# Attention results finished with longer planned lags, and their divisors broadcast by one transfer in place of four

## The chip, the cores and the metric

The kernel runs on one core of one Trainium2 chip. The time is device microseconds (us) of that core. Engines: TensorE (PE) does the matmuls, VectorE (DVE) elementwise work and row reductions, ScalarE (ACT) activations and copies, GpSimd (POOL) some elementwise work and DMA issue, and SyncE (SP) only issues DMAs. Each engine runs its own instructions in program order.

## The reference

x is 2 × 1024 × 512 in fp32. Cut to what matters:

```python
xn = layernorm(x)                                   # over the last 512
q, k, v = split(xn @ w_qkv.T + b_qkv)               # 32 heads of 16
scores = q @ k.T / 4 + slope[h] * (key - S + 1)     # ALiBi
attn   = softmax(where(causal, scores, -1e9))
s = (attn @ v).reshape(B, S, D) @ w_out.T + b_out
h = silu(oct_linear(xn, w_gate)) * oct_linear(xn, w_up)   # 512 -> 1360, ternary octonion weights
g = silu(oct_linear(h, w_down))
out = x + s * g
```

The octonion linear layers use weights rounded to −1, 0 or 1 times a scale, in an 8 × 8 pattern of signed blocks.

## The kernel before

**Units.** Attention is cut into 32 units (b, g, qc): two batches, eight groups of four heads, two halves of 512 queries. A unit has four parts on TensorE: score matmuls with queries on the partitions, of which VectorE takes row maxima (L566, tiles `s` and `s_d`, `left`, `mx`); the maxima turned round and put into `q_stack` as extra rows; score matmuls with keys on the partitions (L682, L701), whose exponentials ScalarE takes into `p` (L69 in the profile, since all engines but TensorE record through one helper at that line); and value matmuls (L720), which add up in the PSUM tile `po`. The values carry a column of ones, so that in each head's 32 rows of `po` row 16 is the softmax sum of its queries. ScalarE copies a finished `po` to `posb`.

**A result's steps.** `finish(b, g, qc)` (L733) returns six steps, written for one unit:
- `sums`: a DMA from SyncE takes the four rows of sums out of `posb` into `l`, 128 partitions × 16 (`l<-posb`);
- `invert`: VectorE takes the reciprocal, `rl`;
- `keep`: a DMA puts `rl` into DRAM as 4 × 512 (`ld<-rl`);
- `spread`: DMAs bring each head's row of 512 factors back to its 32 partitions of `r`, 128 × 512 (`r<-ld`);
- `divide`: VectorE multiplies `posb` by `r`, in place in `r`;
- `store`: a DMA writes `r` to `att` in DRAM (`att<-r`). Later `oT<-att` fetches it for the output projection.

**The order of work.** The program is written out by a planner at build time. It keeps modelled times in ns: `now` for TensorE, `act` and `dve` for the others. In each turn of its main loop it may emit a fill of keys or queries (`try_fill`, four DMAs `k_stack<-sp` or `q_stack<-sp`, SyncE), then one due step of a result (`do_chores`), then a fetch of `oT` (`try_fetch`), then one group of matmuls (`step`). Each step of a result is a triple (emit, cost on VectorE, lag): after it is emitted, the next is due when its modelled end plus the lag has passed:

```python
emit, cost, lag = steps.pop(0)
emit()
end = run_dve(now[0], cost) if cost else now[0]
chores[n] = (end + lag, steps, u)
if not steps:
    stored[units[u]] = end + lag
```

So the lags do not wait on the chip; they decide where in each engine's program the step stands. On the chip an engine waits, at that place, until the step's inputs are there, and what follows it on that engine waits too. SyncE's program also has the loads of x (`xt`), of the query and key weights (`wqr`), the spills `sp<-st` of the projections, and the fills.

**Buffers.** `posb` has two buffers, `l` and `rl` one each. `r` has the tag "ot" with two buffers, which it shares with `md`, the transposed pieces of the down weights (`turn_down`: PE transposes to `ptd`, ScalarE copies `md<-ptd`, GpSimd stores `mw<-md`), made between 120 and 180 us.

**After attention** a feed-forward loop runs (gate and up matmuls `pg`, `pu` at L1455, down matmuls `pd` at L1497). Steps of results that are left by then are emitted one round per pass of that loop.

Of the kernel before, what the change touches and what calls it, by code (L numbers as in the profile page):

```python
# [75 lines left out]
def kernel(  # L76
# [21 lines left out]
    act_, dve_, pool_, sp_ = (  # L98
        InOrder(tc, engine, held) for engine in (nc.scalar, nc.vector, nc.gpsimd, nc.sync)
    )  # L100
# [12 lines left out]
    dram = ctx.enter_context(tc.tile_pool(name="dram", bufs=1, space=DRAM))  # L113
# [111 lines left out]
    for n in range(2):  # L225
        pool_.dma_start(
            out=bqk_sb[n * 64 : n * 64 + 64, 1 - n : 1 - n + 2 * NG],
            in_=bqk.rearrange("(i d) c -> i d c", d=32)[:, 0:HD, :],
# [504 lines left out]
    def finish(b, g, qc):  # L733


        posb = po_tiles.pop((b, g, qc))
        key = f"{b}_{g}_{qc}"
        box = {}

        def sums():  # L740
            box["l"] = wk.tile([P, 16], F32, tag="l", name=f"l_{key}", bufs=1)
            sp_.dma_start(
                out=box["l"],
                in_=posb[HD:P:32, :].rearrange("h (a n) -> h a n", n=16),
            )

        def invert():
            box["rl"] = wk.tile([P, 16], F32, tag="rl", name=f"rl_{key}", bufs=1)
            dve_.reciprocal(box["rl"], box["l"])

        def keep():
            box["dram"] = spill.tile([4, 512], F32, tag="l", name=f"ld_{key}")
            sp_.dma_start(
                out=box["dram"].rearrange("h (a n) -> (h a) n", n=16), in_=box["rl"]
            )

        def spread():
            box["r"] = wk.tile([P, 512], F32, tag="ot", name=f"r_{key}")
            for h in range(4):
                sp_.dma_start(  # L760
                    out=box["r"][32 * h : 32 * h + 32],
                    in_=box["dram"][h : h + 1].to_broadcast([32, 512]),
                )

        def divide():
            dve_.tensor_tensor(box["r"], posb, box["r"], ALU.mult)

        def store():
            sp_.dma_start(out=att[b, g, :, qc * 512 : qc * 512 + 512], in_=box["r"])


        return [
            (sums, 0, 9000),
            (invert, 250, 300),
            (keep, 0, 3500),
            (spread, 0, 7000),
            (divide, 620, 300),
            (store, 0, 4500),
        ]

# [85 lines left out]
    for b in range(B):  # L866
        for hh in range(2):
            n = 2 * b + hh
# [11 lines left out]
        for gp in range(2 - 2 * b, NP):  # L880
            n = b * NP + gp
# [374 lines left out]
    def next_value():  # L1256
        if V[0] == len(vals) or V[0] not in p_ready or not V[0] and S_[0] < head_v:
            return []
        u, n, cell = vals[V[0]]
        last = 4 * units[u][2] + 2  # L1260

        def go():
            value_step(*units[u], n, cell)
            V[0] += 1
            run_pe("V", ready, sum(w * 1.668 + 40 for _, _, w in cell))
            if n == last:
                o_free[0] = run_act(now[0] + START, 480) + END
                chores.append((o_free[0], finish(*units[u]), u))

        ready = max(p_ready[V[0]], o_free[0] if n == 0 else 0)  # L1270

        if n % 2 == 0 and n < last and V[0] + 2 >= E_cell():
            ready = max(ready, p_ready.get(V[0] + 1, HELD) - 800)
        return [(ready, 0, 0, go)] if ready < HELD else []
# [377 lines left out]
```

## Time and profile before

| | |
|---|---|
| median of 3 runs | 1032.09 us (1031.54 to 1032.76) |
| the profiled execution | 1030.97 us |
| its span | 1029.1 us |
| mean granted TensorE clock | 0.991 |
| PE, DVE, ACT, POOL busy | 988.5, 581.4, 490.6, 171.7 us |
| DMA queue of SyncE | 74384 packets, 111.40 MB |
| r<-ld | 128 issues, 64 KB each |

The span runs from the profile's first to its last instruction; the execution's own time has 1.87 us more around it. A line such as `r<-posb,r` names the tile written and the tiles read, without their numbers; times in the timeline count from the start of the span. Busy time of one engine lies beside that of the others. What an engine waited for is put down to what came last. The granted clock is the share of full speed at which TensorE was let run.

### The profile page before, as it was taken

What the parts mean: (1) busy time and instruction counts of PE and PEld (TensorE: products, weight loads), DVE (VectorE), ACT (ScalarE), POOL (GpSimd) and SP (SyncE); (2) the same over time, 40 slices, a digit from 0 to 9 for tenths busy, and PEclk for the clock granted to TensorE, in tenths of its full rate; (3) what the DMA queues carried; (4) which work ended last, traced back from release to release, by engine and by line L of the source; (5) the groups of instructions that cost most, each with busy time, mean ns of one, the idle gap of its engine ahead of it and who ended that gap; (6) DMA issues with size and microseconds to landing.
All of it is one profiled execution on the core that took longest, in us unless ns stands there. A gap on an engine that the chain in (4) does not pass through costs nothing. (4 is left out here: it accounts for less than half of the span.)

```text
span 1029.1 us, 15486 instructions
## 1 busy us (share of the span) xinstructions
PE 988.5 (96%) x5290; PEld 669.1 (65%) x5290; DVE 581.4 (56%) x1726; ACT 490.6 (48%) x942; POOL 171.7 (17%) x289
## 2 busy tenths in 40 slices
PE   8999988999999999899999999989999999999996
PEld 6655645775666676656667656545476678788784
DVE  6588945776577675676766757748251132231312
ACT  4034456756656554456654556556761132232322
POOL 7701023100200200010010000010021133232322
PEclk9999998999999999999999999999999999999998
DMA  5854735244454423433533244532242113030201
GB/s 203 244 150 154 169 129 167 63 131 154 144 150 138 137 66 123 152 109 117 166 95 96 84 130 148 124 100 79 86 148 82 51 66 109 1 123 1 94 29 42
DMA packets 77935, 117.16 MB, mean 114 GB/s; under 512 B 19624, under 2 KB 29488, under 8 KB 77856
## 3 DMA queue, kind: packets, MB, share of 16 engines
q1 hardware_dynamic: 74384, 111.40, 35.1%
q0 software_dynamic: 3424, 4.64, 1.6%
q8 instruction: 42, 0.69, 0.3%
q14 instruction: 37, 0.30, 0.1%
q10 hardware_dynamic: 48, 0.13, 0.0%
HBM read 77.77 MB, written 37.56 MB: 112 GB/s over the span
## 5 line engine op out<-in xcount | busy, mean ns | idle before, releaser
L69 ACT ACTIVATE p<-s 128x512 f32<-128x512 f32 x576 | 319.4, 596 | 183.4 <-PE s L701 105.7
L682 PE MATMUL s<-q_stack,k_stack 128*128 128x512 f32 (+3 forms) x768 | 263.0, 408 | 4.9 <-ACT p L69 4.5
L69 DVE TENSOR_REDUCE left<-s 128x1 f32<-128x512 f32 x256 | 161.4, 681 | 71.2 <-PE s L566 70.9
L682 PEld LDWEIGHTS s<-q_stack,k_stack 128*128 128x128 f32 x768 | 132.4, 191 | 88.3 <-ACT p L69 44.2
L69 DVE CUSTOM_DVE_ANT_0 nowhere<-s_d,mask 128x384 uint8<-128x384 f32 (+2 forms) x384 | 139.6, 419 | 21.4 <-PE s_d L566 20.0
L720 PE MATMUL po<-p,v 128*32 128x512 f32 (+3 forms) x1536 | 142.6, 491 | 2.8 <-ACT p L69 2.8
L566 PE MATMUL s_d<-k_stack,q_stack 126*128 126x384 f32 (+3 forms) x512 | 128.5, 348 | 4.0 <-DVE mx L69 3.6
L479 PE MATMUL pqk<-xnT,wq 128*128 128x512 f32 x256 | 128.3, 601 | 3.2 <-ACT md L69 1.2
L69 POOL DMA_DIRECT2D q_stack<-mr x64 | 31.0, 488 | 558.5 <-ACT mr L69 558.5
L69 DVE SCALAR_TENSOR_TENSOR h<-pu,sc_u,sg 128x512 f32<-128x512 f32 (+1 forms) x44 | 33.0, 750 | 152.2 <-PE pu L1455 146.7
L566 PEld LDWEIGHTS s_d<-k_stack,q_stack 126*128 126x128 f32 x512 | 83.4, 192 | 26.4 <-DVE mx L69 11.2
L69 DVE CUSTOM_DVE_ANT_0 s_d<-s_d,mask 128x512 f32<-128x512 f32 x128 | 85.6, 715 | 21.9 <-PE s_d L566 21.6
L566 PE MATMUL s<-k_stack,q_stack 126*128 126x512 f32 x256 | 86.5, 422 | 7.9 <-DMA q_stack<-sp 5.7
L69 POOL TENSOR_TENSOR hs<-h,hs 128x512 fp32r<-128x512 f32 (+1 forms) x43 | 56.2, 1307 | 211.6 <-ACT hs L69 211.6
L720 PEld LDWEIGHTS po<-p,v 128*32 128x32 f32 x1536 | 43.4, 109 | 72.6 <-issue 57.9
L701 PE MATMUL s<-mask_r,ident_r 128*128 128x256 f32 (+1 forms) x320 | 89.7, 280 | 0.0
L69 ACT ACTIVATE sg<-pg,sc_g 128x512 f32<-128x512 f32 (+1 forms) x44 | 30.2, 687 | 104.4 <-PE pg L1455 104.4
L69 ACT CAST hs<-h 128x512 fp32r<-128x512 f32 (+1 forms) x44 | 27.3, 620 | 84.4 <-DVE h L69 84.4
L439 PE MATMUL pv<-wv,xnT 128*128 128x256 f32 x256 | 65.1, 384 | 0.0
L701 PEld LDWEIGHTS s<-mask_r,ident_r 128*128 128x128 f32 x320 | 61.1, 191 | 2.8 <-issue 1.7
L566 PEld LDWEIGHTS s<-k_stack,q_stack 126*128 126x128 f32 x256 | 47.1, 190 | 23.6 <-issue 5.8
L479 PEld LDWEIGHTS pqk<-xnT,wq 128*128 128x128 f32 x256 | 44.5, 190 | 27.2 <-issue 18.6
(149 smaller groups left out, 1152.0 us busy)
## 6 DMA issues: line engine op xcount, KB each, us to landing
sp<-st SPq DMA_DIRECT2D x32, 512.0 KB
k_stack<-sp SPq DMA_DIRECT2D x128, 128.0 KB
q_stack<-sp SPq DMA_DIRECT2D x128, 128.0 KB
wqr<-in_wqk_dram SPq DMA_DIRECT2D x16, 512.0 KB
r<-ld SPq DMA_DIRECT2D x128, 64.0 KB
att<-r SPq DMA_DIRECT2D x32, 256.0 KB
xt<-in_x_dram SPq DMA_DIRECT2D x16, 256.0 KB
oT<-att SPq DMA_DIRECT2D x32, 128.0 KB
```

The source lines that it names most:

```text
L69: ins = issue(*args, **kwargs)
L439: nc.tensor.matmul(ps[:, 0:256], lhsT=xnT[:, c, b * S + kt * P : b * S + (kt + 1) * P], rhs=wv_tiles[2 * b + hh][:, c, :], start=(c == 0), ...
L479: nc.tensor.matmul(ps, lhsT=wq_tiles[b, gp][:, kt, which, :], rhs=xnT[:, kt, b * S + c * 512 : b * S + (c + 1) * 512], start=(kt == 0), st ...
L566: nc.tensor.matmul(ps, lhsT=q_of(b, g, qc)[0 : NR - 2, h, tl * P : (tl + 1) * P], rhs=k_of(b, g, c)[0 : NR - 2, h, :n], start=True, stop=True,
L682: nc.tensor.matmul(ps[:, c0 : c0 + w], lhsT=k_of(b, g, kt // 4)[0:NR, h, kt % 4 * P : (kt % 4 + 1) * P], rhs=q[0:NR, h, 512 - w : 512], st ...
L701: pe(nc.tensor.matmul(out, lhsT=ident_r, rhs=rhs, start=False, stop=True))
L720: nc.tensor.matmul(po[32 * i : 32 * i + 32, 512 - w : 512], lhsT=v[:, kt, h * VC : h * VC + 32], rhs=p[:, i * part + c0 : i * part + c0 + ...
```

## The change

The four transfers of `spread` become one, with a source whose leading size is 4 (heads), then 32 repeats of a row, then 512. Three planned lags grow: after `invert` from 300 to 2000 ns, after `spread` from 7000 to 8000, after `divide` from 300 to 2500. The planned time from the copy of `po` to `stored` grows from 25.47 to 30.37 us. Each later step so stands later in the engines' programs, and the planner's later choices move with it.

```diff
         def spread():
             box["r"] = wk.tile([P, 512], F32, tag="ot", name=f"r_{key}")
-            for h in range(4):
-                sp_.dma_start(
-                    out=box["r"][32 * h : 32 * h + 32],
-                    in_=box["dram"][h : h + 1].to_broadcast([32, 512]),
-                )
+            sp_.dma_start(
+                out=box["r"],
+                in_=box["dram"].rearrange("h (e n) -> h e n", e=1).to_broadcast([4, 32, 512]),
+            )
...
         return [
             (sums, 0, 9000),
-            (invert, 250, 300),
+            (invert, 250, 2000),
             (keep, 0, 3500),
-            (spread, 0, 7000),
-            (divide, 620, 300),
+            (spread, 0, 8000),
+            (divide, 620, 2500),
             (store, 0, 4500),
         ]
```

## The prediction

> **What bounds the kernel now.** First I read the page's first part, then the chain that ended last.
>
> ```profile
> PE 988.5 (96%) x5290; PEld 669.1 (65%) x5290; DVE 581.4 (56%) x1726; ACT 490.6 (48%) x942; POOL 171.7 (17%) x289
> PE 4%; issue 0%; DVE 0%; ACT 0%; DVEq 0%
> ```
>
> TensorE is busy for 96% of the span; VectorE has nearly half its time free. So an edit of VectorE's and SyncE's steps can gain only what TensorE now idles or runs at a lower clock, and can lose only by making new idle time. The recovered chain covers only the last 4%, so I looked for TensorE's idle time stage by stage.
>
> ```profile
> 100.00:200.00 100.00, 90.02 (x510) 58.45 (x512) 66.23 (x204) 61.20 (x131) 19.19 (x33) 0.95 0.47 135
> 400.00:500.00 100.00, 97.22 (x560) 61.13 (x559) 69.31 (x219) 57.59 (x106) 5.78 (x16) 0.98 0.43 132
> 835.00:1029.10 194.10, 183.99 (x806) 148.68 (x804) 53.26 (x60) 52.30 (x82) 55.64 (x42) 0.99 0.16 55
> ```
>
> Columns: stretch, length, busy time of PE, PEld, DVE, ACT and POOL, granted clock, DMA share, GB/s. From 100 to 200 us 10 us are idle at a clock of 0.95: that stretch is the softest. The last stretch is the feed-forward loop, one matmul stream behind another; there only its start, 749.79 us (the first pg), can move. It lasts 279.3 us in both programs: by the timeline the last stores land 7 us or more before their oT is fetched.
>
> Next, who waits for the five steps of a chain, by the view of waits (total, times, longest) and then SyncE's queue:
>
> ```profile
> DVE r L69 <- DMA r<-ld: 11.1, 5, 4.1
> PE s L566 <- DMA q_stack<-sp: 5.7, 3, 3.4
> ACT md L69 <- DMA mw<-md: 8.5, 3, 3.3
> SPq L69 <- DVE rl L69: 49.1, 16, 6.8
> SPq L69 <- DVE r L69: 33.5, 15, 6.8
> ```
>
> Of 32 divides 5 wait for their factors. The timeline (start, length, engine; in brackets idle time and releaser) shows what two of them cost:
>
> ```profile
> 91.46 1.98 SPq L69 DMA_DIRECT2D r<-ld  x4
> 95.11 0.69 DVE L69 TENSOR_TENSOR r<-posb,r 128x512 f32<-128x512 f32 x1 [2.73 <-DMA r<-ld]
> 96.46 0.50 PE L566 MATMUL s<-k_stack,q_stack 126*128 126x512 f32 x1 [2.20 <-DVE left L69]
> ...
> 416.87 1.82 SPq L69 DMA_DIRECT2D r<-ld  x4
> 423.49 0.69 DVE L69 TENSOR_TENSOR r<-posb,r 128x512 f32<-128x512 f32 x1 [4.13 <-DMA r<-ld]
> 424.90 0.50 PE L566 MATMUL s_d<-k_stack,q_stack 126*128 126x384 f32 x2 [2.66 <-DVE mx L69]
> ...
> 684.25 0.96 PE L566 MATMUL s<-k_stack,q_stack 126*128 126x512 f32 x3 [3.39 <-DMA q_stack<-sp]
> ```
>
> While a divide waits, the row maxima queued behind it on VectorE wait too, and the score matmuls lack a bank. The first costs TensorE 2.20 us. The second costs 2.66 us and then clock:
>
> ```profile
> 425.00:430.00 5.00, 5.00 (x21) 4.52 (x22) 3.85 (x19) 1.74 (x3) 0.00 (x0) 0.66 0.60 185
> ```
>
> 5 us at 0.66 lose 1.7 us, so this wait costs 4.4 in all. The third gap is a late fill of q_stack and cost no clock.
>
> **The parts of the change.** *One transfer for four.* The rows:
>
> ```profile
> L69 SPq DMA_DIRECT2D r<-ld x128: 303/419/1354, 91.5 to 762.2; - x128
> L69 SPq DMA_DIRECT2D l<-posb x32: 555/587/642, 68.1 to 752.2; - x32
> L69 SPq DMA_DIRECT2D att<-r x32: 320/338/474, 95.8 to 767.4; - x32
> ```
>
> Four issues at the median of 419 ns are 1.68 us per chain. For the new one the bounds are 0.34 (the plain store) and 0.64 us (the longest l<-posb); I take 0.59, as l<-posb too has an access pattern led by four rows. That frees 32 × 1.09 = 35 us of SyncE's queue, which isn't the bound: worth nothing itself, but fills behind it go out earlier.
>
> *How soon it lands.* Now 3.65 us from first issue to the divide (91.46 to 95.11), 1.67 after the fourth issue ended. The mean packet takes 35.1% × 16 × 1029.1 us / 74384 = 78 ns (an estimate from the page's queue row). The 128 rows of 2 KB are 8 packets on each of 16 engines (0.6 us) or, if the transfer is split only over its four leading rows, 32 on each of four (2.5 us). So it lands 0.59 + 1.67 = 2.3 us after issue at best, 2.3 + 1.9 = 4.2 at worst: −1.4 to +0.5 against now. I take the worst, because the broadcast stands with 4 outermost. Either way the extra 1 us of planned lag covers it.
>
> [...] No row here shows a broadcast led by four.
>
> *Longer lags.* The planned chain was 9 + 0.55 + 3.5 + 7 + 0.92 + 4.5 = 25.47 us and becomes 30.37. It needs no more buffers: a unit comes every (752.2 − 68.1)/31 = 22.1 us, posb has two buffers (44 us) and is held some 26, l and rl some 10. The gain meant is that SyncE's keep and store no longer stand waiting (49.1 and 33.5 us above) ahead of fills; off the path, except for the fills.
>
> *What moves where.* The built programs differ in order on every engine. I followed the three gaps into the new order:
> - Gap at 96.46: the divide stands two row maxima later, and TensorE has four score groups and two value groups before it needs that bank. Gain 2.2 (0 to 2.2).
> - Gap at 424.90: these factors are now requested ahead of the 1 MB of wqr loads that they followed (414.93). A landing of 3.65 in place of 6.6 us ends the wait. Gain 4.4 (0 to 4.4).
> - Gap at 684.25: the fill now stands ahead of one store, but still behind the transfers that take until 673.3 to issue. Gain 0.4 (0 to 3.4).
> [...]
> - Stretch 120 to 180 us, where the down weights are transposed: md copies and r tiles share the two buffers of tag "ot". Copies there already wait for each other:
>
> ```profile
> 136.53 0.58 ACT L69 CAST md<-ptd 128x512 fp32r<-128x512 f32 x1 [3.28 <-DMA mw<-md]
> 140.24 0.53 ACT L69 CAST md<-ptd 128x256 fp32r<-128x256 f32 x2 [3.12 <-DMA mw<-md]
> ```
>
> One buffer turns round in 3.7 us. In the new order r_0_1_0 takes its buffer after md_0_4, so SyncE waits there for md_0_4's store, and the store of r_0_0_1, for which md_0_8 waits, is queued behind that. Against it, the exponentials of unit (0,1,1) come some ten places earlier and fill ScalarE's idle time. From −5 (half of the 10 us idle goes) to +6; taken: +1.
> - New waits: the 32 divides meet other neighbours. Today's waits cost 2.2 + 4.4 = 6.6. With lags longer by 1 us I take +2.5 (0 to 6.6).
>
> **The sum**: −2.2 − 4.4 − 0.4 + 1 + 2.5 = −3.5 against the profiled execution's own 1030.97 us (span 1029.1 and 1.87 around it) gives 1027.5. That execution lay 1.12 below the median of 1032.09, so as a median: 1028.6. This case's own range: 1024 to 1032.
>
> **Rivals.** *Slower: the shared buffers.* md_0_8 waits for md_0_4's store (3.7), then the issues of r_0_1_0 and att (0.59 + 0.34), then that store's landing (about 4, as a landing took 3.65): 8.6 us after md_0_4 in place of 3.7. TensorE's next transposes need its PSUM bank: 4.9 idle and 1.7 of clock, +6.6; a second crossing of this kind, at md_2_0, adds up to 3. With the gains: −7.0 + 2.5 + 6.6 to 9.6 = +2.1 to +5.1, median 1034 to 1037; 1041 if the new waits cost all of 6.6. It eats up the gain from a stall of 4.5 us in that stretch, and can be measured as a loss from 6.5. For it: the 3.28 and 3.12 waits. Against it: TensorE has score and value groups to do first.
>
> *Slower: four engines carry too much.* If the factors' 32 packets hold up the fills that share these engines, each by up to 1.9 us, and two fills in the eight groups are as tight as the one at 684, +3.8, and clock once, 1.7: −7.0 + 2.5 + 3.8 + 1.7 = +1.0, and +5.4 if the 4.4 isn't won: median 1033 to 1037. For it, fills were late three times (5.7 us); against it, the DMA share is 0.43.
>
> *No change: the waits move.* Other divides and fills wait in place of these, costing again about 6.6: median 1031 to 1033. For it: both gaps come from where the planner happens to put a step, not from its lags as such.
>
> **How the numbers follow.** Chances: forecast 0.50, shared buffers 0.24, four engines 0.11, no change 0.15. About 0.2% (2 us) is what this kernel's measurement can tell from no change. The range: 1021 (the soft stretch gives its 5 us and little new waits) to 1040. Faster 0.50, same 0.16, slower 0.34.
>
> **What would show it.** Right: r<-ld x32 at about 0.59 us each on SyncE, landing in 4.2; no TensorE idle before 96.5 and 425, and the clock near 425 at 1.00; the first pg near 746. Wrong: ACT md waits well over 8.5 us and a lower share of PE from 100 to 200 (under 88); new DVE r waits above 11.1; or q_stack waits above 5.7.
>
> [...]

## The result, and the profile after

The changed kernel is slower: 1035.02 us median of 15 runs (1032.61 to 1036.98) against 1032.29 of 15 runs before; the ratio is 1.0031, 95% interval 1.002 to 1.0042. The forecast was 1028.6, faster. The time lies in the predicted range, and where two of the rivals were priced: the shared buffers (1034 to 1037) and the four engines (1033 to 1037). The experiments show that the shared buffers are one half of the story; the other half is a term that the prediction had set to nothing.

The profiled execution took 1036.54 us (span 1034.8, clock 0.985). It and the profiled execution before (1030.97) lie 5.6 us apart, twice the 2.7 between the medians; the account of stages below is of these two executions, and its single terms are no surer than that. The windows (stretch, length, busy time of PE, PEld, DVE, ACT, POOL, clock, DMA share, GB/s) first:

```profile
100.00:200.00 100.00, 81.85 (x467) 55.12 (x466) 59.65 (x192) 54.55 (x118) 19.20 (x33) 0.90 0.46 132
425.00:430.00 5.00, 5.00 (x33) 2.55 (x32) 2.95 (x16) 1.97 (x4) 0.00 (x0) 1.00 0.75 268
170.00:175.00 5.00, 5.00 (x26) 4.04 (x29) 1.66 (x9) 4.26 (x10) 1.57 (x3) 0.58 0.26 76
```

The wait at 425 us is gone and its clock is whole, as forecast. The soft stretch got worse: TensorE is busy for 81.85 us there in place of 90.02, at a clock of 0.90 in place of 0.95. The waits (total, times, longest) and the new transfer's row:

```profile
DVE r L69 <- DMA r<-ld: 15.2, 5, 4.1
ACT md L69 <- DMA mw<-md: 13.4, 5, 4.7
ACT md L69 <- DMA att<-r: 9.4, 1, 9.4
```

```profile
L69 SPq DMA_DIRECT2D r<-ld x32: 512/553/746, 91.4 to 766.9; - x32
```

The transfer issues in 0.55 us (0.59 was taken). But the divides wait 15.2 us for it, more than the 11.1 before, in spite of the longer lag. And a copy of md now waits 9.36 us for a store of r. Here is that place in the timeline, ScalarE's copies, SyncE's queue and TensorE's gaps:

```profile
143.49 0.59 ACT L69 CAST md<-ptd 128x512 fp32r<-128x512 f32 x1 [2.17 <-DMA mw<-md]
153.43 0.53 ACT L69 CAST md<-ptd 128x256 fp32r<-128x256 f32 x2 [9.36 <-DMA att<-r]
...
147.22 0.52 SPq L69 DMA_DIRECT2D r<-ld  x1
147.79 0.47 SPq L69 DMA_DIRECT2D att<-r  x1
...
154.36 1.46 PE L373 MATMUL ptd<-ident_r,m_d 128*128 128x128 f32 x4 [5.72 <-ACT m_d L69]
169.02 2.44 PE L373 MATMUL ptd<-ident_r,m_d 128*128 128x128 f32 x8 [5.06 <-ACT m_d L69]
```

r_0_1_0 waits on SyncE until 147.22 for its buffer, which md_0_4 has just left; the store of r_0_0_1 stands behind it, although its divide (139.30, 0.69 us long) ended at 140.0; md_0_8 wants that store's buffer; and ScalarE's signed copies (m_d), for the next transposes, stand behind md_0_8.

Where the time went, stage by stage, from the idle time in brackets on TensorE and, per stretch of 5 us, busy time × (1 − clock):

| stage, us | idle before → after | lost to clock |
|---|---|---|
| 0 to 60 | 7.6 → 7.3 | 0 → 0 |
| 60 to 100, and the clock after it | 2.2 → 1.5 | 0 → 1.6 |
| 100 to 200 | 9.8 → 18.0 | 3.8 → 6.1 |
| 200 to 450 | 3.8 → 0.5 | 1.7 → 0 |
| 450 to 600 | 0 → 1.3 | 0 → 0 |
| 600 to 760 | 6.4 → 4.9 | 0 → 1.5 |

That is 3.7 us more idle time and 3.7 more lost to clock. The first pg moved by only 4.7 (749.79 to 754.50): some 2.7 us of TensorE's other time went. The feed-forward loop takes 280.3 us in place of 279.3.

### The profile page after: what moved, and what is told of

Same layout as the page of the kernel before. It is cut to its first block, busy times and chain, and to the rows that moved or that the text cites. A ratio compares the mean times of both kernels' runs of the same rounds, so it can differ in the third digit from the quotient of the medians.

```text
span 1034.8 us, 15321 instructions
## 1 busy us (share of the span) xinstructions
PE 989.5 (96%) x5290; PEld 669.0 (65%) x5290; DVE 581.7 (56%) x1726; ACT 493.6 (48%) x942; POOL 172.0 (17%) x289
## 5 line engine op out<-in xcount | busy, mean ns | idle before, releaser
L682 PE MATMUL s<-q_stack,k_stack 128*128 128x512 f32 (+3 forms) x768 | 268.5, 414 | 4.7 <-ACT p L69 4.3
L69 DVE CUSTOM_DVE_ANT_0 s_d<-s_d,mask 128x512 f32<-128x512 f32 x128 | 86.1, 714 | 22.5 <-PE s_d L566 21.7
L566 PE MATMUL s<-k_stack,q_stack 126*128 126x512 f32 x256 | 88.8, 423 | 5.5 <-DVE left L69 2.8
L720 PEld LDWEIGHTS po<-p,v 128*32 128x32 f32 x1536 | 42.7, 110 | 69.9 <-issue 60.5
L479 PEld LDWEIGHTS pqk<-xnT,wq 128*128 128x128 f32 x256 | 45.0, 191 | 26.2 <-issue 18.3
```

The lines of the kernel that those rows point to most:

```text
L69: ins = issue(*args, **kwargs)
L479: nc.tensor.matmul(ps, lhsT=wq_tiles[b, gp][:, kt, which, :], rhs=xnT[:, kt, b * S + c * 512 : b * S + (c + 1) * 512], start=(kt == 0), st ...
L566: nc.tensor.matmul(ps, lhsT=q_of(b, g, qc)[0 : NR - 2, h, tl * P : (tl + 1) * P], rhs=k_of(b, g, c)[0 : NR - 2, h, :n], start=True, stop=True,
L682: nc.tensor.matmul(ps[:, c0 : c0 + w], lhsT=k_of(b, g, kt // 4)[0:NR, h, kt % 4 * P : (kt % 4 + 1) * P], rhs=q[0:NR, h, 512 - w : 512], st ...
L720: nc.tensor.matmul(po[32 * i : 32 * i + 32, 512 - w : 512], lhsT=v[:, kt, h * VC : h * VC + 32], rhs=p[:, i * part + c0 : i * part + c0 + ...
```

## The experiments

Theory A: r and md collide in their shared buffers. Theory B: the one transfer runs on few engines, lands late, and the divides wait. All ratios are to the kernel before, run on the same chip; the changed kernel itself was not run again beside them, so 1.0031 stands for it. Each kernel differs from the changed kernel or the one before by the lines shown.

**Taking the collision away.** Run e1, the changed kernel with:

```diff
-        md = wk.tile([P, 4, P], F32R, tag="ot", name=f"md_{kp}_{first}")
+        md = wk.tile([P, 4, P], F32R, tag="oT", name=f"md_{kp}_{first}")
```

> The changed kernel with the md copies of the down weights in the two buffers of tag oT, which lie idle at that time, so that md copies and r tiles no longer share buffers. Theory A (shared buffers): ScalarE's wait of 9.4 us for a store of r goes; TensorE's busy share of 100 to 200 us rises from 82 to 90 or more; the time falls by 6 to 10 us from 1035 to 1025 to 1029. Theory B (the one transfer lands late on four engines, and that is the loss): the time stays within 2 us of 1035, and the waits of VectorE for r stay near 15 us.

Measured: 1024.58 us, ratio 0.9898 (0.9873 to 0.9923), 1.3% below the changed kernel. The wait for a store of r is gone, and the stretch:

```profile
100.00:200.00 100.00, 92.69 (x529) 61.25 (x529) 68.90 (x215) 63.50 (x134) 19.21 (x33) 0.93 0.49 137
```

Theory A holds for this part. But the divides still wait, 16.2 us in 7 waits, so B isn't refuted.

Run e2 takes only the collision's first link away, by one number for one unit:

```diff
-            (divide, 620, 2500),
+            (divide, 620, 300 if (b, g, qc) == (0, 0, 1) else 2500),
```

> The changed kernel with one number set back for one unit: the lag after divide of unit (0,0,1) is 300 again in place of 2500, so that the store of r_0_0_1 stands ahead of the transfer r_0_1_0 on SyncE. Theory A (the store queued behind a transfer that waits for its buffer): the wait of 9.4 us for that store goes, md_0_8 starts less than 6 us after md_0_4, and the time falls by 4 to 9 us, to 1026 to 1031. Theory B (late landing on four engines): 1035 within 2 us.

Measured: 1030.57 us, ratio 0.9971 (0.9956 to 0.9986). md_0_8 now starts 4.43 us after md_0_4, in place of 9.94:

```profile
143.78 0.59 ACT L69 CAST md<-ptd 128x512 fp32r<-128x512 f32 x1 [2.17 <-DMA mw<-md]
148.21 0.53 ACT L69 CAST md<-ptd 128x256 fp32r<-128x256 f32 x2 [3.84 <-DMA mw<-md]
163.72 2.43 PE L373 MATMUL ptd<-ident_r,m_d 128*128 128x128 f32 x8 [5.13 <-ACT m_d L69]
```

The gap of 5.72 us is gone, the second one of some 5 stays. So the store queued behind a waiting transfer cost about 0.6%. What e1 gained beyond that is likely the copies' waits for each other's stores, which e2 leaves in place (4.72 us ahead of the gap at 169 in the changed kernel).

**The change's two halves.** Run e3 is the kernel before with the new `spread` alone, run e4 the kernel before with the three new lags alone (both as in the diff of the change).

> The kernel before with the one transfer alone, all lags as before. Theory A: its order has r_0_1_0 behind md_1_0 as before, so no long md wait; the time within 2 us of 1032, plus 0 to 2 for divides that wait longer. Theory B: the one transfer lands some 1.5 us later than the four did, while the lag is still 7000, so the divides wait for r more often than before (over 15 us in all) and the time is at least 1035.

> The kernel before with the three longer lags alone, four transfers kept. Theory A: r_0_1_0 stands between md_0_4 and the store of r_0_0_1 as in the changed kernel, so the 9 us wait of ScalarE is there and the time is 1033 to 1037. Theory B: the four transfers land in 3.65 us, the longer lag hides them, and the time is 1028 to 1032.

Measured: e3 1044.93 us, ratio 1.0099 (1.0074 to 1.0124); e4 1027.79 us, ratio 0.9945 (0.9926 to 0.9965). Both go B's way in time (e4 a little below B's range). In e3, where no such collision stands, the divides wait:

```profile
DVE r L69 <- DMA r<-ld: 29.4, 11, 5.4
98.03 0.65 PE L566 MATMUL s<-k_stack,q_stack 126*128 126x512 f32 x1 [4.04 <-DVE left L69]
427.13 0.79 PE L566 MATMUL s_d<-k_stack,q_stack 126*128 126x384 f32 x2 [3.43 <-DVE mx L69]
```

The two gaps of before (2.20 and 2.66) became 4.04 and 3.43. In e4 the collision is there, with a wait of 7.29 us, and still the kernel gains, since the gaps at 96 and 425 are both gone. So the lags are worth −0.55%, with the collision that they bring already in it, and the one transfer +0.99% (+0.86% beside the new lags, e4 to the changed kernel). From first issue to a divide that waited for it took 3.65 us for four transfers (527.30 to 530.95 in e4) and 5.08 for one (533.58 to 538.66 in the changed kernel). Over all divides that waited it was 3.65 to 3.83 in e4 (three) and 5.08 to 7.43 in the changed kernel (five).

**Both costs away.** Run e5 has four transfers, the new lags and md in tag oT; run e6 is the kernel before with md in tag oT.

> Four transfers, the three longer lags, md copies in the buffers of tag oT. If the two costs found so far (one transfer in place of four: ratio 1.0031 against 0.9945; shared buffers: 1.0031 against 0.9898) are separate, both go: 1.0031 - 0.0086 - 0.0133 = 0.981, about 1013 us beside a kernel before of 1033. If the late landing costs mostly through the shared buffers, the two overlap and the ratio is 0.986 to 0.990, as md apart alone gave.

> The kernel before with md copies in the buffers of tag oT, four transfers and old lags kept. If shared buffers cost the kernel before little (its ScalarE waited 8.5 us in all for md stores, and TensorE was idle 9.8 us from 100 to 200), the ratio is 0.994 to 0.998. If they cost it as much as the changed kernel (13 us), it is 0.987, and the collision is no part of what the change brought.

Measured: e5 1016.18 us, ratio 0.984 (0.9818 to 0.9862), the fastest of all. The two costs nearly add (0.981 was their sum, just below the interval). With md apart the one transfer costs 0.6% (e1 against e5), and with four transfers sharing the buffers costs about 1% (e4 against e5). e6 1030.92 us, 0.9977 (0.9961 to 0.9993): the sharing cost the kernel before only 0.2%, so the collision is of the change's making, through its order. In e5 the divides wait little:

```profile
DVE r L69 <- DMA r<-ld: 3.3, 2, 1.8
```

**The leading size as a dose.** Run e7: md apart, new lags, and

```diff
+            for h in range(0, 4, 2):
+                sp_.dma_start(
+                    out=box["r"][32 * h : 32 * h + 64],
+                    in_=box["dram"][h : h + 2]
+                    .rearrange("h (e n) -> h e n", e=1)
+                    .to_broadcast([2, 32, 512]),
+                )
```

> Two transfers of two heads each in place of one of four, with the new lags and md apart (to be held beside one transfer, 0.9898, and four). If the leading size sets the number of engines that carry a transfer, two transfers led by 2 run on two engines, 64 packets of 80 ns on each: 5.1 us in place of 2.5, so the factors land 2 to 3 us later than with one transfer, the divides wait for r more than 16 us in all, and the ratio is 0.993 to 1.002. If it is only that one large transfer lands later than several small ones, two lie between one and four: VectorE waits less than 16 us and the ratio is below 0.990.

Measured: 1045.64 us, ratio 1.0126 (1.0102 to 1.0151), slower than both four (0.984) and one (0.9898):

```profile
DVE r L69 <- DMA r<-ld: 39.7, 12, 6.2
L69 SPq DMA_DIRECT2D r<-ld x64: 487/504/773, 91.5 to 778.3; - x64
```

From first issue to the waiting divide took 8.04 us (532.27 to 540.31). So here the landing followed neither the number of transfers nor their size, but the leading size: 3.65, 5.08 and 8.04 us for a leading 32, 4 and 2. Here is a microsecond in which the factors travel, for a leading 32 (e4), 4 (the changed kernel) and 2 (e7); the last but one column is the mean busy share of the 16 DMA engines:

```profile
528.00:529.00 1.00, 1.00 (x8) 0.90 (x6) 1.00 (x3) 0.00 (x0) 0.00 (x0) 1.00 0.58 109
536.50:537.50 1.00, 1.00 (x6) 0.71 (x5) 0.00 (x0) 0.90 (x3) 0.00 (x0) 1.00 0.26 102
537.00:538.00 1.00, 0.12 (x1) 0.00 (x0) 0.00 (x0) 1.00 (x2) 0.00 (x0) 1.00 0.13 49
```

Four of 16 engines are a share of 0.25, two are 0.125; the 0.58 of e4 takes more than four. The shares of 0.26 and 0.13 so fit four and two busy engines; which ones carried the transfer, no view shows.

**Hiding the late landing.** Run e8: one transfer, md apart, `(spread, 0, 12000)`. Run e9: the same with a second buffer for rl. Run e13: e9 with four transfers.

> One transfer, md apart, and the lag after spread 12000 in place of 8000, so that the divide stands 4 us further back in VectorE's program. If the cost of the one transfer is that divides wait for it, VectorE's waits for r fall from 16.2 us to under 5 and the time falls to within 3 us of four transfers with md apart. If the cost is that 32 packets on each of four engines hold up the fills that share them, the time stays within 2 us of one transfer with md apart (0.9898).

Measured: 1024.57 us, ratio 0.9917 (0.989 to 0.9943). The divides' waits fell to 5.4 us, but nothing was gained on e1. A new wait took their place:

```profile
290.43 0.25 DVE L69 RECIPROCAL rl<-l 128x16 f32<-128x16 f32 x1 [4.92 <-DMA ld<-rl]
291.39 0.79 PE L566 MATMUL s_d<-k_stack,q_stack 126*128 126x512 f32 x1 [3.64 <-DVE mx L69]
```

The only rl buffer was still held by a keep that had queued behind 4.32 us of q_stack issues and 2.5 us of waiting on SyncE.

> As the run with one transfer, md apart and a lag of 12000 after spread, with a second buffer for rl; the order of every engine is the same instruction for instruction. In that run one reciprocal waited 4.92 us for the store of the rl before it, TensorE stood 3.64 us at 291 us and ran at 0.59 and 0.73 of its clock after it: 3.64 + 5 x (0.41 + 0.27) = 7.0 us. If late landing costs only through the divides that wait for it, this gap was all that the longer lag still lost, and the ratio falls from 0.9917 to 0.985, level with four transfers (0.984). If four busy engines also hold up other transfers, it stays at 0.989 or more.

Measured: 1024.86 us, ratio 0.9925 (0.9908 to 0.9943). The gap at 291 fell to 1.81 us, the time didn't: the first reading, that this gap was all that was left to win, failed. The second, 0.989 or more if four busy engines also hold up other transfers, fits the time, but so does a cost of the longer lag itself.

> Four transfers, md apart, the lag after spread 12000 and two rl buffers: the kernel of the last run on the lag with four transfers in place of one. If the lag of 12000 itself costs what was left (later steps colliding with other things), the ratio is 0.990 to 0.994, as with one transfer (0.9925). If the four busy engines cost it, the ratio is 0.982 to 0.986.

Measured: 1019.49 us, ratio 0.987 (0.9845 to 0.9896), between the two expectations. The longer lag may cost some 0.3% itself (0.984 with 8000; the intervals overlap), and one transfer in place of four a further half per cent, with divides that wait 7.9 us in all (e9) against 3.9 (e13). That is as much as with the lag of 8000 and md apart (0.6%, e1 against e5), although the divides waited 16.2 us there. So the longer lag took away waits for r and won nothing of the transfer's cost; where that cost then lies is open.

**Narrow transfers that nobody waits for.** To e5, run e14 adds behind the four transfers of each unit

```diff
+            sp_.dma_start(
+                out=spare,
+                in_=x[0:4, :].rearrange("h (e n) -> h e n", e=1).to_broadcast([4, 32, 512]),
+            )
```

and run e15 `sp_.dma_start(out=spare, in_=x[0:P, :])`. The latter is as plain as the store `att<-r` issued at 97.63 in the changed kernel, 128 rows of 2 KB too, behind which the DMA share was 1.01 from 98.5 to 99.

> The best kernel so far (four transfers, new lags, md apart; 0.984) with one more transfer in each unit, behind the four: four rows of x broadcast to 128 x 512 in a spare DRAM tile that nothing reads, so 128 packets of 2 KB led by four rows. It costs SyncE some 0.55 us per unit and carries the load of the one transfer, but no one waits for it. If narrow transfers hold up others, 0.990 or more; if only the waiting for r costs, 0.983 to 0.987.

> The same with the spare transfer as 128 plain rows of x, spread over all engines: same bytes, the issue of a plain 128-row transfer. The control for the narrow one: 0.983 to 0.987 under either theory. The difference between the two is what narrowness costs others.

Measured: 0.9876 (0.985 to 0.9901) and 0.9847 (0.982 to 0.9874), 1020.13 and 1018.23 us; the intervals overlap, so the 1.9 us isn't settled by time. The trace tells more. SyncE's waits for the landing of ld between 60 and 750 us (total, times, longest), in e5, e14 and e15 in this order:

```profile
SPq L69 <- DMA ld<-rl: 42.7, 21, 4.9
```

```profile
SPq L69 <- DMA ld<-rl: 54.8, 20, 5.9
```

```profile
SPq L69 <- DMA ld<-rl: 43.5, 20, 4.8
```

The 32 narrow transfers that nobody waits for made SyncE wait 12 us longer for others, 32 wide ones of the same bytes 1 us. The other kernels with these lags fall in line: over the same stretch SyncE waits 41.6 us for ld in e4 and 42.4 in e13 (four transfers), 47.9 in the changed kernel and 53.3 in e1 (one), 72.2 in e7 (two). In e14 a fill of q_stack came late, too:

```profile
303.34 0.70 PE L566 MATMUL s<-k_stack,q_stack 126*128 126x512 f32 x2 [2.87 <-DMA q_stack<-sp]
```

**Which lag.** Runs e10, e11 and e12 are the kernel before with one of the three lags: `(invert, 250, 2000)`, `(spread, 0, 8000)`, `(divide, 620, 2500)`. Run e16 is e11 with md in tag oT.

> The kernel before with the lag after invert alone at 2000. If the gain of the lags is that SyncE no longer stands at keep ahead of fills, its waits for rl fall well below 49 us, the q_stack wait of 3.39 us shrinks, and the ratio is 0.995 to 0.998. If the gain is that divides find r landed, this lag brings nothing: 0.999 to 1.003.

> The kernel before with the lag after spread alone at 8000. If the gain of the lags is that divides find r landed, the waits of 2.20 us (at 96) and 2.66 us with 1.7 of clock (at 425) go, VectorE's wait for r falls from 11 to about 4 us, and the ratio is 0.993 to 0.996. Otherwise 0.999 to 1.003.

> The kernel before with the lag after divide alone at 2500. It moves only the stores of r. If the gain of the lags is that SyncE no longer stands at a store ahead of fills (33.5 us of waits for r), the ratio is 0.995 to 0.998; otherwise 0.999 to 1.003, since both long waits of TensorE come before a store is due.

> The kernel before with the lag after spread at 8000 and md apart, nothing else. If the gains are separate: 0.9951 + 0.9977 - 1 = 0.9928. If the three lags together make a better order with md apart, it stays there and does not come near 0.984.

Measured: e10 1.0008 (0.9991 to 1.0025), e11 0.9951 (0.9933 to 0.9969), e12 1.0011 (0.9998 to 1.0025), e16 0.9908 (0.988 to 0.9937). The gain of the lags is the spread lag's. In e10 SyncE's wait for rl fell from 49.1 to 29.3 us, in e12 that for r from 33.5 to 18.3, and neither moved the time. But SyncE's wait for the landing of ld rose, from 21.7 us to 38.2 in e10 and 29.0 in e12, so much of the waiting only changed its place, and that it was off the path isn't shown. In e11 the gap at 425 is gone and the one at 684 is 1.23 us, though the one at 96 stayed, at 2.56, and the divides wait 8.3 us in place of about 4, against what its expectation says. e16 holds the sum of e11 and e6 (0.9928) within its interval. But e5, with all three lags, is at 0.984: with md apart the other two lags are worth something, and how was not tried.

## Why the prediction was wrong

- **"Either way the extra 1 us of planned lag covers it"** is the step that failed first: the one transfer was priced at nothing and cost 0.86 to 0.99%, some 9 to 10 us (0.6% with md apart). Its landing was put at 2.3 to 4.2 us after issue; it was 5.1 or more. Part of that is the transfer's own traffic, estimated at 2.5 us on four engines: in slices of half a us it runs, with an 8 KB `ld<-rl` in it, from between 534.5 and 535 to between 538 and 538.5, over 3 us, at a DMA share of at most 0.31. More important, the lag is counted from where the planner thinks the issue is. On the chip the transfer at 91.39 was issued right behind a fill of 2.44 us, and the divide's turn came 2.1 us after it (96.91, less 3.38 of waiting). Of 8 us of planned lag 2.1 were left. 27 of the 32 divides were covered; the five others waited 15.2 us.

```profile
88.90 2.44 SPq L69 DMA_DIRECT2D q_stack<-sp  x4
91.39 0.55 SPq L69 DMA_DIRECT2D r<-ld  x1
96.91 0.69 DVE L69 TENSOR_TENSOR r<-posb,r 128x512 f32<-128x512 f32 x1 [3.38 <-DMA r<-ld]
98.25 1.99 PE L566 MATMUL s<-k_stack,q_stack 126*128 126x512 f32 x3 [1.50 <-DVE left L69]
```

- **The gap at 96**: 2.2 was to be gained. 0.7 was, and the remaining 1.50 cost 1.6 of clock: a loss of 0.9. With four transfers (e4) the gap is gone, as forecast.
- **The gap at 425**: 4.4 forecast, all of it came.
- **The gap at 684**: 0.4 forecast, 2.5 came (0.86 was left).
- **The stretch of the shared buffers** is the second step that failed, and no smaller: +1 was taken from −5 to +6; it was 8.2 of idle time and 2.3 of clock, 10.5, beyond the range of the term and of the rival's 6.6 to 9.6. The rival's place and chain were right: md_0_8 came 9.94 us after md_0_4 where 8.6 was worked out, and TensorE stood 5.72 where 4.9 was. The second gap of 5.06 was not the crossing at md_2_0 that was priced at up to 3, but a copy that waited 4.72 us for the store of another md. The argument against it, that TensorE had other groups to do first, was worth nothing, as ScalarE's queue stood behind md_0_8.
- **New waits**: +2.5 taken; the gap of 1.27 at 540, the 1.5 of clock at 720 to 730 and 1.0 in the feed-forward loop make 3.8.
- **TensorE's other time**: no term of the sum. Some 2.7 us of it went that are neither idle nor clock; what saved them is not shown.
- **The gain meant for the longer lags**, that SyncE's keep and store no longer stand waiting, did not come: in the changed kernel SyncE waited 68.0 us for rl (49.1 before), 38.6 for r (33.5) and 47.9 for ld (21.7).
- **The second rival** (four engines hold up fills) was not what cost the time: in the changed kernel `s` waited 1.7 us for fills of q_stack, less than the 5.7 before. That narrow transfers held up others is so in e14 (54.8 us of waits for ld against 42.7 in e5, and one fill that TensorE waited 2.87 us for). What the rival left out is the divides themselves.

So both causes stand in the prediction, the one as a rival and the other as a landing that the lag would cover, and the chances stood on the wrong side because they were read as alternatives to the gain. They act together: −0.55% for the lags with their collision, +0.86% for the transfer, and of the 1.3% that e1 won back, most was of the change's own making. That the lags alone (e4, −0.55%) came near the forecast of −0.34% is partly luck: the shared buffers cost them about 1% there, and they won more than was forecast elsewhere, as e5 (−1.6%) shows.

## What to carry to other kernels

Before merging transfers, look at the leading size of the merged access pattern: here a broadcast led by 4 landed 1.4 us later than four led by 32 (5.08 against 3.65), and broadcasts led by 4 also made others late (12 us more of waits in e14). A planned lag is no cover until the trace shows where the step really stands in the queue; take the time from issue to the consumer's turn from the timeline. And where a step on a DMA queue may wait for a buffer, as the transfer at 147.22 did, ask what behind it frees the next one.

## What was not expected of the hardware

The granted clock was lower after some short gaps and not after others: after 1.50 us of idle time at 98 it was at 0.75 for 5 us, after 2.56 at 97 in e11 at 1.00, after 1.27 at 540 at 1.00, after 3.39 at 684 in the kernel before at 1.00. In e1, 1.41 us of idle time at 529 were followed by 5 us at 0.69. So in these runs a gap's cost couldn't be read from its length alone. The dip had one size in the two that were read in slices of half a us: 0.50 from 426.4 to 429.8 in the kernel before, after a gap of 2.66, and 0.50 from 99.1 to 102.5 in the changed one, after 1.50. That is 3.4 us at 0.50, or 1.7 us lost, in the second more than the gap.

The price of the narrow transfers was also paid by others: in e14, 12 us more of waits for a small unrelated transfer than in e5 (54.8 against 42.7), from 32 narrow transfers of 256 KB.
